# Graph network in one kernel: PSUM operands and TensorE transposes in layer 0's edge loop, two PSUM tiles and a later last product at the end of layer 2, and earlier loads at the seams

## The chip, the cores and the metric

The kernel runs on one core of a Trainium2 chip, as one program. The metric is the device time of that core in microseconds (us), the median of several executions. Executions of the same kernel differ by some 0.1 to 0.3% on one chip. All runs told here are of the fast state: none is over 1.5% above the fastest of its kernel. Names of engines in the profile: PE is TensorE's matmuls, PEld its weight loads, DVE is VectorE, ACT ScalarE, POOL GpSimd, SP SyncE.

## The reference

A graph network of four layers over 4,096 nodes of 512 features and 65,536 edges. Each layer adds its result to `x` after a layer norm and a relu.

```python
h = relu(layernorm(x)); x = x + softmax(gat(h, adj, W, a))          # layer 0: 8 heads of 64, attention over the edges
h = relu(layernorm(x)); x = x + gcn(h, weight)                      # layer 1: degree-normed sum over edges, product, relu
h = relu(layernorm(x)); x = x + edge_mlp(h, edge_attr, W1 .. W4)    # layer 2, below
h = relu(layernorm(x)); x = x + relu(gcn(h @ W.T + b))              # layer 3

def edge_mlp(x):                                                    # layer 2
    hid = mish(concat(x[src], x[dst], edge_attr) @ W1 + b1)         # per edge
    agg = segment_sum(mish(hid @ W2 + b2), dst)                     # per edge, summed per node
    u   = mish(concat(x, agg) @ W3 + b3)                            # per node from here
    y   = x + u @ W4 + b4
    return layernorm(y) * gamma + beta
```

## The kernel before

Edges are sorted by node and taken in tiles of 128. The rows at the far ends of a tile's edges are gathered from DRAM by an indirect DMA that GpSimd issues, weighted, and added per node by a TensorE product with a one-hot matrix. In layer 0 a group is eight tiles. Three parts matter here. The first is **layer 0's loop**, which also needs each edge's own scores. It gets them from a product with the transposed one-hot, built on VectorE from a loaded table, `places`.

```python
def source_parts(g, places):
    oh_t = ep.tile([P, GT * P], BF16, name="oh_t")
    nc.vector.tensor_scalar(oh_t, places, col_i, None, op0=OP.is_equal)
    # ... of = three bf16 parts of the block's node scores ...
    for j in range(GT):
        for k in range(3):
            nc.tensor.matmul(e_ps[:, j]..., oh_t[:, j * P:(j + 1) * P], of[:, j // 2, k, :], start=k == 0, stop=k == 2)

def weights(g, rows, u):
    nc.vector.tensor_mul(rows[:, :, D:D + H], u, s_new[...])        # weights, into SBUF
    return one_hots(ep, s_loc, at(g), GT)                           # compare row_i (SBUF) with s_loc

def weigh(j, rows):                                                 # two tiles
    # ... ScalarE scales two of the eight heads ...
    nc.vector.tensor_mul(g, g, two[:, :, D:D + VH]...to_broadcast([P, 2, VH, F]))   # all operands in SBUF
```

The second is the **end of layer 2**, a software pipeline over 16 groups of 256 nodes:

```python
for p in range(groups + 3):
    if now(p):      # load rows of h2, transpose them and acc's on TensorE, copy out on ScalarE (h_t, a_t)
    if now(p - 1):  # product with w3
        u_ps = lps.tile([P, KC, R * P], F32, name="u_ps", bufs=1)
        for m in range(KC):
            for k in range(2 * KC):
                nc.tensor.matmul(u_ps[:, m, :], w3_sb[...], ..., start=k == 0, stop=k == 2 * KC - 1)
            nc.scalar.activation(zu[:, m, :], u_ps[:, m, :], AF.Identity, bias=b3_sb[:, m:m + 1])
    if now(p - 2):  # product with w4, o_ps, added to h2's rows
    if now(p - 3):  # last product: transposes of h3, copy to h3_t, product with wl, store to ztab
    if now(p - 2):  # layer norm of y, x3, layer norm of x3 -> h3
```

The third is the **seams**: what GpSimd and the loads do between layer 1 and the messages of layer 2 (edge ends are gathered only once layer 1 is over), and between the messages and layer 2's end (its weights and rows are loaded once all of the messages' memory is free).

Of the kernel before, what the change touches and what calls it, by code (L numbers as in the profile page):

```python
# [19 lines left out]
P = 128  # L20
# [13 lines left out]
def kernel(  # L34
# [54 lines left out]
    col_i = const.tile([P, 1], F32, name="col_i")  # L89
    nc.gpsimd.iota(col_i, pattern=[[0, 1]], base=0, channel_multiplier=1,  # L90
                   allow_small_or_imprecise_dtypes=True)
# [27 lines left out]

    loc_rows = dram.tile([G * P, P], BF16, name="loc_rows")  # L120
# [9 lines left out]
    def by_order(o, pool, ppool):  # L130
# [117 lines left out]
        nc.vector.tensor_tensor(limit, til[:1, :], limit, op=OP.is_gt)  # L248
        nc.vector.reduce_max(over, limit, axis=AX.X)
# [66 lines left out]
        low_p = pool.tile([P, G, P], BF16, name="low_p")  # L316
        nc.vector.tensor_copy(low_p, loc)
        nc.sync.dma_start(loc_rows.rearrange("(g p) c -> p g c", p=P), low_p)
# [132 lines left out]
    def one_hots(pool, loc, t0, n):  # L451

        oh = pool.tile([P, n, P], F32, name="oh")
        nc.vector.tensor_tensor(oh, row_i.unsqueeze(1).to_broadcast([P, n, P]),
                                loc[:, t0:t0 + n].unsqueeze(2).to_broadcast([P, n, P]), op=OP.is_equal)
        return oh
# [221 lines left out]
    def attend(first, last):  # L678
        @with_exitstack
        def run(ctx):  # L680
            ep = ctx.enter_context(tc.tile_pool(name="edge", bufs=2))
            eps = ctx.enter_context(tc.tile_pool(name="edge_ps", bufs=2, space=PSUM))
            groups = (last - first) // GT
# [11 lines left out]
            def fetch_places(g):  # L695
                places = ep.tile([P, GT * P], BF16, name="places", bufs=3)
                nc.sync.dma_start(places, loc_rows[at(g):at(g) + GT].rearrange("t c -> (t c)").partition_broadcast(P))
                return places

            def source_parts(g, places):  # L700

                oh_t = ep.tile([P, GT * P], BF16, name="oh_t")
                nc.vector.tensor_scalar(oh_t, places, col_i, None, op0=OP.is_equal)
                e_ps = eps.tile([P, GT, 2, H], F32, name="e_ps")
                of = ep.tile([P, GT // 2, 3, 2 * H], BF16, name="of")
                for j in range(0, GT, 2):
                    b = block_of(nc.scalar, bi_s, at(g) + j)
                    nc.scalar.copy(of[:, j // 2], node3[:, ds(b, 1)].rearrange("p b k c -> p (b k) c"))
                for j in range(GT):
                    for k in range(3):  # L710
                        nc.tensor.matmul(e_ps[:, j].rearrange("p c h -> p (c h)"), oh_t[:, j * P:(j + 1) * P],
                                         of[:, j // 2, k, :], start=k == 0, stop=k == 2)
                return e_ps

            def scores(rows, e_ps):
                u = ep.tile([P, GT, H], F32, name="u")
                nc.vector.tensor_add(u, e_ps[:, :, 0, :], rows[:, :, D:D + H])
                nc.vector.scalar_tensor_tensor(u, u, 0.2, u, op0=OP.mult, op1=OP.max)
                nc.vector.tensor_sub(u, u, e_ps[:, :, 1, :])

                nc.vector.tensor_scalar(u, u, SAFE_RANGE + 10.0, None, op0=OP.min)
                nc.scalar.activation(u, u, AF.Exp)
                nc.scalar.copy(rows[:, :, D + H:], one2.unsqueeze(1).to_broadcast([P, GT, 2]))
                return u

            def weights(g, rows, u):
                nc.vector.tensor_mul(rows[:, :, D:D + H], u,
                                     s_new[:, at(g):at(g) + GT].unsqueeze(2).to_broadcast([P, GT, H]))
                return one_hots(ep, s_loc, at(g), GT)

            def weigh(j, rows):
# [6 lines left out]
                g = two[:, :, :VH * F].rearrange("p t (h f) -> p t h f", h=VH)  # L738
                nc.vector.tensor_mul(g, g, two[:, :, D:D + VH].unsqueeze(3).to_broadcast([P, 2, VH, F]))
# [14 lines left out]
            rows, places, done = {}, {}, {}  # L754
            for g in range(-3, groups):
                now = lambda k: 0 <= k < groups
                if now(g + 3):
                    rows[g + 3] = fetch(g + 3)
                if now(g + 2):
                    places[g + 2] = fetch_places(g + 2)  # L760
                if now(g + 1):
                    e_ps = source_parts(g + 1, places.pop(g + 1))
                ps = None
                for j in range(0, GT, 2):
                    if now(g):
                        weigh(j, rows[g])
                        if ps is not None:
                            keep(g, j - 2, ps)
                        ps = add_up(g, j, rows[g], done[g])
                    if j == 2 and now(g + 1):  # L770
                        u = scores(rows[g + 1], e_ps)
                if now(g + 1):
                    done[g + 1] = weights(g + 1, rows[g + 1], u)
                if now(g):
                    keep(g, GT - 2, ps)
                    del rows[g], done[g]
# [81 lines left out]
    class Between:  # L858


        AHEAD, APART = 3, 8
# [13 lines left out]
        def block(self, b):  # L875
# [30 lines left out]
            for k0, tab in ((0, ptab), (KC, qtab)):  # L906
# [5 lines left out]
                pq = pool.tile([P, D], F32, name="pq", bufs=3)  # L912
# [29 lines left out]

    with tc.tile_pool(name="between", bufs=1) as bp, tc.tile_pool(name="between_ps", bufs=1, space=PSUM) as bps, \
# [3 lines left out]
                  between.follow)(0, TS_MAIN)  # L947
        between.the_rest()
    for flag in (more, late):
        with tc.If(nc.values_load(flag[:, 0:1], min_val=0, max_val=1) > 0):  # L950
            if flag is more:
                sum_edges(ytab, s_dst, s_loc, bi_s, 2)(TS_MAIN, TS)
            with tc.tile_pool(name="redo", bufs=1) as bp, tc.tile_pool(name="redo_ps", bufs=1, space=PSUM) as bps:
                Between(bp, bps).the_rest()
# [6 lines left out]

    half_pi = const.tile([P, 1], F32, name="half_pi")
# [3 lines left out]
    nc.gpsimd.memset(acc[:, NB // 2:, :D], 0.0)  # L966

    with ExitStack() as l2:
        wp = l2.enter_context(tc.tile_pool(name="l2_w", bufs=1))
# [7 lines left out]
        def messages(ctx, first, last):  # L977
            lp = ctx.enter_context(tc.tile_pool(name="l2", bufs=2))
            lps = ctx.enter_context(tc.tile_pool(name="l2_ps", bufs=2, space=PSUM))
            U = 4  # L980
            NG = (last - first) // U


            HALF = DE + 3
# [5 lines left out]
            def fetch_ends(i):  # L990
                eg = lp.tile([P, U // 2, 2 * HALF], F32, name="eg", bufs=4)
                for j in range(U):
                    t = first + i * U + j
                    nc.gpsimd.indirect_dma_start(  # L994
                        out=eg[:, j // 2, (j % 2) * HALF:(j % 2 + 1) * HALF], out_offset=None,
                        in_=aug.rearrange("e c -> (e c)").unsqueeze(0),
                        in_offset=bass.IndirectOffsetOnAxis(ap=d_eid[:, t:t + 1], axis=1))
                return eg

            def fetch_rows(eg):  # L1000
                pg = lp.tile([P, U, D], F32, name="pg", bufs=4)
                qg = lp.tile([P, U, D], F32, name="qg", bufs=3)
                for j in range(U):
# [4 lines left out]
            def keep_ends(i, eg):  # L1008
                r = slice(first + i * U, first + (i + 1) * U)
# [5 lines left out]
            def turn_attributes(eg):  # L1015
                et_ps = lps.tile([P, U // 2, P], F32, name="tr_ps")
                for j in range(U // 2):
                    nc.tensor.transpose(et_ps[:, j, :], eg[:, j, 3:3 + 2 * DE], ident)
                et = lp.tile([P, U // 2, P], F32, name="et")
# [3 lines left out]
            def attribute_products(et):  # L1023
                made = []
                for j in range(U):
# [23 lines left out]




            fetched, rows, h, z = {}, {}, {}, {}
            ctx.enter_context(tc.manual_schedule(engines=ENGINES))
            for i in range(-3, NG + 2):
                now = lambda k: 0 <= k < NG
                if now(i + 3):
                    fetched[i + 3] = fetch_ends(i + 3)
# [3 lines left out]
                if now(i - 1):  # L1062
                    hh = h.pop(i - 1)
                    zz = z[i - 1] = lp.tile([P, U, D], F32, name="z", bufs=2)
# [12 lines left out]
                if now(i - 2):  # L1077
                    oh = one_hots(lp, d_loc, first + (i - 2) * U, U)
                    mz = z.pop(i - 2)
                    t = lp.tile([P, U, D], F32, name="t", bufs=1)  # L1080
# [3 lines left out]
                if now(i - 1):  # L1084
                    ps = second_product(h_t[1])
                    nc.vector.tensor_add(zz[:, 1, :], ps, b2_bc)  # L1086
                if now(i + 1):
# [4 lines left out]
                if now(i):  # L1092
# [5 lines left out]
                if now(i + 1):  # L1098
                    for j in range(2, U):
# [4 lines left out]
                if now(i - 2):  # L1104
                    nc.scalar.activation(t, t, AF.Sin, bias=half_pi, scale=-2.0)
                    for j in range(0, U, 2):
                        nc.vector.tensor_mul(mz[:, j:j + 2], mz[:, j:j + 2], t[:, j:j + 2])  # L1107
                if now(i):
# [5 lines left out]
                for j in range(U):  # L1114
                    if now(i - 2):
                        add_message(first + (i - 2) * U + j, oh[:, j, :], mz[:, j, :])
                    if now(i) and j == 1:
                        nc.vector.tensor_mul(pg[:, 2:], pg[:, 2:], qg[:, 2:])

        in_two(1, TD_MAIN, TD, messages)  # L1120
# [3 lines left out]
    with ExitStack() as end:  # L1124
        wp = end.enter_context(tc.tile_pool(name="l2_end_w", bufs=1))
        lp = end.enter_context(tc.tile_pool(name="l2_end", bufs=2))
        lps = end.enter_context(tc.tile_pool(name="l2_end_ps", bufs=2, space=PSUM))
        w3_sb = load_w(wp, "w3_sb", w3)
        w4_sb = load_w(wp, "w4_sb", w4)
        wl_sb = load_w(wp, "wl_sb", w_l3t)  # L1130
# [193 lines left out]
```

## Time and profile before

The median of the kernel before was 6323.75 us in its first three runs. I use stages between landmarks that both traces have, since the same work then stands on both sides:

| stage, between starts in the trace | before, us |
|---|---|
| to layer 0's first product of the loop (`sum_ps`) | 297.3 |
| layer 0's loop, first to last `sum_ps`, 68 groups | 755.4 |
| last `qtab` store (layer 1 over) to the messages' first product (`m_ps`) | 53.7 |
| messages, first to last `m_ps` | 2919.5 |
| last `m_ps` to the first product of layer 2's end (`u_ps`) | 46.6 |
| layer 2's end, first `u_ps` to the last store of `ztab` | 585.4 |
| from there to the end of the span | 694.2 |

Each row is the difference of two starts. The view of one tile gives them: for each operation the count, the shortest, median and longest duration in ns, then the first and the last start.

```profile
L745 PE MATMUL sum_ps<-rows,oh x2176: 381/383/782, 297.3 to 1052.7; 128*128 128x261 f32 x198
```

1052.7 less 297.3 is the loop's 755.4 us, 11.1 a group. In a group's line, "x529 | 572.6, 1082 | 161.2 <-issue 130.1" means 529 instructions, busy 572.6 us, 1,082 ns each, and an idle engine for 161.2 us in front of them, of which 130.1 with no cause that the profile shows.

### The profile page before, as it was taken

How to read it: one execution, taken by the hardware profiler on the slowest of the kernel's cores; microseconds unless marked ns; L12 is line 12 of the kernel's file. 1: busy time of each engine (PE TensorE's matmuls, PEld its weight loads, DVE VectorE, ACT ScalarE, POOL GpSimd, SP SyncE). 2: the span in 40 equal slices, each digit the busy share in tenths (PEclk: the TensorE clock that was granted, in tenths of full speed). 3: DMA queues.
4: the chain of work that ended last, by engine and by line, in shares of the span. 5: the costliest groups of instructions: out<-in, count | busy, mean ns of one | idle time of the engine just before them, and what ended most of it. 6: DMA issues, size and time to landing. Idle time of an engine off the chain costs nothing. (4 is left out here: it accounts for less than half of the span.)

```text
span 6333.0 us, 65970 instructions
## 1 busy us (share of the span) xinstructions
PE 5615.5 (89%) x18462; PEld 2821.0 (45%) x18462; DVE 4171.6 (66%) x7268; ACT 2953.4 (47%) x4025; POOL 3262.4 (52%) x3295
## 2 busy tenths in 40 slices
PE   6688887899998899999999999999999789968877
PEld 4366665344443344444444444444444465632222
DVE  7577778466654666666666666666666445556666
ACT  3144444311110677777777777777777533310000
POOL 1277774276774755555555555555555000027776
PEclk9799999999999999999999999999999899989999
DMA  8777775587785433333333333333333211137777
GB/s 227 175 217 214 217 216 180 183 244 234 240 235 171 126 99 102 103 103 101 100 101 99 99 103 103 103 100 100 101 99 100 78 47 63 61 109 210 225 242 220
DMA packets 401315, 926.61 MB, mean 146 GB/s; under 512 B 137462, under 2 KB 137462, under 8 KB 400918
## 3 DMA queue, kind: packets, MB, share of 16 engines
q0 software_dynamic: 230976, 721.66, 39.6%
q1 hardware_dynamic: 169942, 200.40, 10.0%
q8 instruction: 159, 2.61, 0.2%
q14 instruction: 238, 1.95, 0.1%
HBM read 818.71 MB, written 103.11 MB: 146 GB/s over the span
## 5 line engine op out<-in xcount | busy, mean ns | idle before, releaser
L448 PE MATMUL m_ps<-w_sb,h_t 128*128 128x512 f32 x4224 | 1905.3, 599 | 31.2 <-ACT h_t L1037 31.2
L813 PE MATMUL sum_ps<-g,oh 128*128 128x512 f32 x2144 | 1075.0, 617 | 157.7 <-DMA g<-ztab,d_src 94.3
L448 PEld LDWEIGHTS m_ps<-w_sb,h_t 128*128 128x128 f32 x4224 | 770.9, 190 | 983.3 <-issue 790.8
L459 POOL DMA_INDIRECT qg<-qtab,eg x528 | 503.3, 953 | 990.1 <-ACT h_t L1037 845.2
L459 POOL DMA_INDIRECT g<-ztab,d_src x528 | 514.2, 974 | 867.5 <-DMA x_end<-x 706.9
L469 DVE TENSOR_TENSOR acc<-acc,sum_ps 128x512 f32 x800 | 549.8, 687 | 535.6 <-PE sum_ps L813 453.3
L459 POOL DMA_INDIRECT g<-ytab,s_dst x544 | 541.0, 994 | 402.8 <-DMA x_mid<-x 187.1
L813 PEld LDWEIGHTS sum_ps<-g,oh 128*128 128x128 f32 x2144 | 376.8, 192 | 796.4 <-DVE acc L469 346.6
L459 POOL DMA_INDIRECT rows<-htab,s_dst x544 | 587.1, 1079 | 209.3 <-issue 134.4
L994 POOL DMA_INDIRECT eg<-aug,d_eid x528 | 568.9, 1078 | 161.2 <-issue 137.1
L1037 ACT COPY h_t<-tr_ps 128x512 f32<-128x512 f32 x528 | 283.8, 589 | 777.2 <-PE tr_ps L1035 777.2
L745 PE MATMUL sum_ps<-rows,oh 128*128 128x261 f32 x2176 | 556.0, 412 | 58.0 <-PE sum_ps L745 41.4
L459 POOL DMA_INDIRECT pg<-ptab,eg x528 | 509.2, 964 | 160.9 <-issue 160.3
L745 PEld LDWEIGHTS sum_ps<-rows,oh 128*128 128x128 f32 x2176 | 430.4, 203 | 162.4 <-PE sum_ps L745 67.5
L1047 PE MATMUL small_ps<-z,oh 128*128 128x512 f32 x1056 | 477.5, 595 | 8.4 <-DVE z L1107 8.4
L1086 DVE TENSOR_TENSOR z<-m_ps,b_bc 128x512 f32<-128x512 f32 x132 | 91.3, 692 | 467.4 <-PE m_ps L448 467.4
L469 DVE TENSOR_TENSOR acc<-acc,small_ps 128x512 f32 x528 | 360.8, 683 | 31.5 <-PE small_ps L1047 4.1
L1262 ACT ACTIVATE t_end<-acc,dis 128x512 f32<-128x512 f32 x32 | 23.0, 721 | 664.7 <-DVE acc L469 664.7
L1072 DVE TENSOR_TENSOR z<-m_ps,b_bc 128x512 f32<-128x512 f32 x132 | 91.3, 692 | 352.2 <-PE m_ps L448 352.2
L1047 PEld LDWEIGHTS small_ps<-z,oh 128*128 128x128 f32 x1056 | 201.3, 191 | 263.6 <-issue 221.8
L1107 DVE TENSOR_TENSOR z<-z,t 128x1024 f32<-128x1024 f32 x264 | 310.2, 1216 | 8.2 <-ACTq L474 4.8
L1035 PEld LDWEIGHTS tr_ps<-ident,pg 128*128 128x128 f32 x2112 | 247.8, 141 | 151.2 <-issue 120.2
(266 smaller groups left out, 8471.7 us busy)
## 6 DMA issues: line engine op xcount, KB each, us to landing
aug<-row SPq DMA_DIRECT2D x32, 560.0 KB, 4.7
places<-loc_rows SPq DMA_DIRECT2D x68, 256.0 KB, 4.0
xt<-in_x_dram SPq DMA_DIRECT2D x16, 1024.0 KB, 6.7
row<-in_edge_attr_dram SPq DMA_DIRECT2D x32, 512.0 KB, 6.7
rows<-htab,s_dst POOLq DMA_INDIRECT x544, 3.8
g<-ytab,s_dst POOLq DMA_INDIRECT x544, 4.3
eg<-aug,d_eid POOLq DMA_INDIRECT x528, 2.7
pg<-ptab,eg POOLq DMA_INDIRECT x528, 3.6
```

Of the source, the lines that this page charges most:

```text
L448: nc.tensor.matmul(ps, h_t[:, k, :], w_sb[:, k0 + k, :], start=start and k == 0, stop=stop and k == KC - 1)
L459: nc.gpsimd.indirect_dma_start(out=dst_ap, out_offset=None, in_=table, in_offset=bass.IndirectOffsetOnAxis(ap=idx, axis=0))
L469: nc.vector.tensor_add(into, into, ps)
L745: nc.tensor.matmul(ps[:, c, :HW], oh[:, j + k, :], rows[:, j + k, c * HW:(c + 1) * HW], start=k == 0, stop=k == 1)
L813: nc.tensor.matmul(ps, oh[:, j + k, :], g[:, j + k, :], start=k == 0, stop=k == pair - 1)
L994: nc.gpsimd.indirect_dma_start(out=eg[:, j // 2, (j % 2) * HALF:(j % 2 + 1) * HALF], out_offset=None, in_=aug.rearrange("e c -> (e c)").un ...
L1035: nc.tensor.transpose(h_ps[:, k, :], h[:, j, k * P:(k + 1) * P], ident)
L1037: nc.scalar.copy(h_t, h_ps)
L1047: nc.tensor.matmul(ps, oh, m, start=True, stop=True)
L1072: nc.vector.tensor_add(zz[:, 0, :], ps, b2_bc)
L1086: nc.vector.tensor_add(zz[:, 1, :], ps, b2_bc)
L1107: nc.vector.tensor_mul(mz[:, j:j + 2], mz[:, j:j + 2], t[:, j:j + 2])
```

## The change

Its intent: shorten layer 0's loop by giving VectorE's large operations a PSUM operand and taking the transposed one-hots from TensorE; keep TensorE fed at layer 2's end; and start loads and gathers earlier at the seams. The core of the diff, with cuts marked:

```diff
 # layer 0's loop
+both_ps = kept.tile([P, P + 2 * GT * H], F32, name="both_ps")    # PSUM: row ids, and two slots of weights
+nc.scalar.copy(ids_ps, row_i)
-places = ep.tile([P, GT * P], BF16, name="places", bufs=3)        # and its load
-nc.vector.tensor_scalar(oh_t, places, col_i, None, op0=OP.is_equal)
+nc.tensor.transpose(t_ps[:, k, :], oh[:, j + k, :], ident)        # eight a group, then two ScalarE copies to bf16
-for k in range(3): nc.tensor.matmul(e_ps[:, j]..., of[:, j // 2, k, :], ...)      # 24 products of 16 columns
+nc.tensor.matmul(e_ps[:, j]..., of[:, j // 2]..., start=True, stop=True)          # 8 products of 48 columns
+nc.vector.reduce_sum(near, e_ps..., axis=AX.X)
-nc.vector.tensor_mul(g, g, two[:, :, D:D + VH]...)
+nc.vector.tensor_mul(part, part, w_ps[:, g % 2, j:j + 2, :VH]...)
 # ... and a new order of the steps of three groups ...
 # seam ahead of the messages
+begun = {i: fetch_ends(0, i) for i in range(3)}                   # edge ends, while layer 1 still runs
-nc.gpsimd.memset(acc[:, NB // 2:, :D], 0.0)
+nc.scalar.activation(acc[:, NB // 2:, :D], zero..., AF.Copy)
 # ... first multiply after Sin ahead of the next group's additions; one branch fewer after layers 1 and 3 ...
 # layer 2's end
+own = dict(reuse_waits="tile")                                    # pools wait for the bytes of a tile, not for all
+# w3 in halves between the first two groups' rows, wl last
-u_ps = lps.tile([P, KC, R * P], F32, name="u_ps", bufs=1)
+u_ps = [lps.tile([P, KC // 2, R * P], F32, name="u_ps") for _ in range(2)]
-for m in range(KC):
+for m in (0, 2, 1, 3):
+nc.gpsimd.tensor_add(h[p], h[p], b4_bc...)                        # was on VectorE; so with beta
-if now(p - 3):                                                    # last product
+if now(p - 4):                                                    # ... at the end of the body
 # ... norms with 13 tiny operations instead of 15, scale and gamma in one pass ...
```

## The prediction

> **What bounds the kernel now.** I first cut the span into stages with the table of busy time by stretch. Its columns: length; then busy us and instructions (x) of TensorE, its weight loads, VectorE, ScalarE and GpSimd; granted clock; DMA share; GB/s. The rows are layer 0's edge loop, layer 1's edges, layer 2's messages, layer 2's end and layer 3's edges.
>
> ```profile
> 280.00:1065.00 785.00, 607.90 (x3808) 476.06 (x3808) 598.20 (x1041) 337.55 (x1502) 587.05 (x544) 0.93 0.75 212
> ...
> 1222.00:2050.00 828.00, 739.37 (x1829) 331.81 (x1829) 497.32 (x1082) 107.36 (x243) 557.02 (x557) 0.96 0.75 228
> 2050.00:5030.00 2980.00, 2877.84 (x8712) 1334.57 (x8712) 2030.50 (x2772) 2157.64 (x1720) 1576.69 (x1579) 0.99 0.34 100
> 5030.00:5660.00 630.00, 522.44 (x1937) 341.10 (x1938) 308.72 (x842) 192.84 (x224) 12.53 (x13) 0.94 0.20 70
> 5660.00:6333.00 673.00, 542.32 (x1040) 163.08 (x1039) 449.84 (x683) 22.99 (x32) 501.68 (x515) 0.99 0.75 223
> ```
>
> The messages, nearly half of the time, keep TensorE 97% busy, and the diff leaves their steady loop alone. The two other edge loops are not touched either. What can move is layer 0's loop, layer 2's end, and the seams on both sides of the messages.
>
> In layer 0's loop no engine looks full, so I read its groups of instructions by line, then the instructions in order of time, then the clock microsecond by microsecond.
>
> ```profile
> L459 POOL DMA_INDIRECT rows<-htab,s_dst x529 | 572.6, 1082 | 161.2 <-issue 130.1 <-PE sum_ps L745 14.6 <-DVE u L719 7.9
> ```
>
> ```profile
> 612.64 0.54 DVE L703 TENSOR_SCALAR oh_t<-places,col_i 128x1024 bf16<-128x1024 bf16 x1
> ...
> 613.10 1.81 DVE L739 TENSOR_TENSOR rows<-rows 128x768 f32<-128x768 f32 x2
> ...
> 613.24 1.62 POOL L459 DMA_INDIRECT rows<-htab,s_dst  x1 [0.30 <-issue]
> ...
> 617.66 0.95 POOL L459 DMA_INDIRECT rows<-htab,s_dst  x1 [0.30 <-DMA rows<-htab,s_dst]
> 617.86 0.70 DVE L752 TENSOR_TENSOR acc<-acc,sum_ps 128x522 f32 x1 [2.95 <-PE sum_ps L745]
> ```
>
> ```profile
> 615.00:616.00 1.00, 1.00 (x3) 0.71 (x3) 0.00 (x0) 0.00 (x0) 0.83 (x1) 0.50 0.90 243
> ```
>
> GpSimd issues 8 gathers a group, each 1.082 us plus a gap of 161.2/529 = 0.305: 8 x 1.387 = **11.1 us**. The loop's period is the same: its first and last products start 755.2 us apart over 68 groups, 11.1 each. So GpSimd's issue sets the pace. A gather takes 0.95 us, but 1.62 beside VectorE work that reads SBUF only, and it ends when that work does; beside an addition that reads PSUM (L752) it stays at 0.95. TensorE loses too: after its idle time before the small score products the clock is 0.50 for some 3 us of each group.
>
> In layer 2's end TensorE is the bound, with named holes; the seam ahead of it waits for loads that begin only when the messages are over:
>
> ```profile
> L1191 PE MATMUL u_ps<-h_t,w_sb 128*128 128x256 f32 x512 | 128.6, 395 | 30.0 <-ACT zu L1193 30.0
> ...
> L448 PE MATMUL o_ps<-wl_sb,h_t 128*128 128x512 f32 x256 | 117.6, 613 | 17.9 <-ACT h_t L1171 17.9
> ...
> L1169 PE MATMUL tr<-ident,h 128*128 128x128 f32 x128 | 18.8, 292 | 24.3 <-DVE h L1161 24.3
> ```
>
> ```profile
> 5047.70 1.94 PE L1169 MATMUL tr<-ident,h_sb 128*128 128x128 f32 x8 [22.41 <-DMA h_sb<-h]
> ```
>
> **What the Trainium skill says.** "GPSIMD Engine Reference", section 1: GpSimd's SBUF interface is shared with VectorE, with contention from instructions in a 2-port mode or with two SBUF inputs. The lines above agree (1.62 against 0.95). "VectorE: DVE Perf Modes", "Why PSUM operands drop a tier": a PSUM operand holds fp32 work to one element a cycle, which `tensor_tensor` has anyway. The trace agrees: 522 elements with a PSUM operand take 694 ns, 768 from SBUF alone 951, both near 1 ns an element beyond a fixed part. "TensorE: Matmul & The Clock Gate", Part 1: an idle window of about 3.4 us halves the clock. Here 0.50 lasts about that long. Its Part 4 says that transposes do not count as busy in the same way; in the messages, with 18 transposes a group, the clock is 0.99.
>
> **Layer 0's loop.** Removed: the load of `places`, the 0.54 us comparison and 16 of 24 score products. Moved to PSUM operands: the one-hot comparison (1.22 us) and four weighings (0.95 each), so that 5.5 us of locks a group are nearly gone. Added: eight transposes (1.04 us for eight, by the messages' rows), two ScalarE copies, a reduction. GpSimd then needs 8 x (0.945 + 0.305) = 10.0 us. TensorE warm: 32 product records at 3.76 us per 16 = 7.5; transposes 1.04; eight score products about 0.45 (24 narrower ones take 0.76; estimate). And one wait: in the changed order VectorE does, between the scores and the last product, the reduction (about 0.55, estimate), four small ops (0.9), a weighing (0.95) and an addition (0.69), 3.1 us, beside a product of 1.9: 1.2 idle. Sum **10.2**. VectorE's own sum stays near 8.9. TensorE's 10.2 is the larger: 0.9 x 68 = **-60 us**.
>
> **Seam before the messages.** Ahead of the first row gather (2053.9) GpSimd spends 6.9 us on clearing `acc` and 8 x 1.25 on edge-end gathers. Both go: three groups of ends are fetched before the seam, ScalarE clears. But all engines must pass the second branch, and ScalarE's clear of 8192 elements takes about 7.6 us (an estimate: four times the 1.9 us that its passes over 2048 take in the messages). I take -10. The first multiply after Sin now precedes the second group's additions: Sin ended at 2075.85, the multiply began at 2084.19, -8. Sum **-18**.
>
> **Seam after them.** The last addition into `acc` ends at 5026.05, the first product of the end starts at 5053.4. With weights and rows in place earlier, two rounds of transpose (1.0 to 1.9) and copy (1.02) remain, some 5 us: **-22**.
>
> **Layer 2's end.** Two PSUM tiles by turns put another 3.6 us product over each 0.56 us wait: -28 of the 30.0. The last product a group later fills the waits for the final norms: -24. Against it, one more iteration early on has nothing to cover the load of rows (4.65 us seen before a transpose at 5104): +5. The 17.9 us wait for `h_t` stays, as the product still follows its own transposes. Shorter norms and the bias additions on GpSimd lie beside TensorE (VectorE is 55% busy): 0. Sum **-47**. One branch fewer at the end: -3.
>
> Sum: -60 - 18 - 22 - 47 - 3 = -150, so 6323.75 - 150 = **6174 us** (2.4%).
>
> **Rivals.** (1) GpSimd stays the bound: if the few small ops still lock it, or the shared pace slips, the loop is at 10.6 rather than 10.2: -33 instead of -60, 6200. For: it is the pace now, and 10.0 is close. (2) TensorE goes cold in the new loop, because transposes do not count: some 1.7 us a group, no gain there, 6235. Against: 0.99 in the messages. (3) VectorE and TensorE overlap better than my order of work and GpSimd's 10.0 binds, and layer 2's end hides `h_t` as well: 6140. (4) DMA takes over: the gathers move 8 x 128 x 2080 bytes in 10.2 us, 209 GB/s, under the 212 that the stage moves now; unlikely.
>
> **Range and chances.** Layer 0's loop is the wide term: -20 if a part of its gain is lost to a new wait, -75 if the loop runs at GpSimd's 10.0. The other three were worked out from single waits, and I allow each 8 us, partly cancelling. From 6174 that gives 6138 to 6212. Faster by over 2% needs under 6197, 23 us above my number, so three of the four terms may miss a third of their size before it fails: 0.83. Slower by over 2% would need layer 0's loop at 14 us a group, for which I see no mechanism.
>
> **What would show it.** Gathers of `rows` near 0.96 us instead of 1.08; a period of 10.2 with a granted clock near 0.98; TensorE's largest wait there before the last product, on VectorE. First message product some 36 us after the last store of `qtab` is issued, not 54; first product of the end within 8 us of the last addition; waits on `zu` near zero, those on `h_t` still near 18. I am wrong if gathers are short but the period stays at 11, or if the clock in the loop falls under 0.93.

## The result, and the profile after

The changed kernel took **6144.28 us** (median of 4 runs, 6142.68 to 6148.06) against 6326.26 for the kernel before on the same chip: ratio 0.9714 (95% interval 0.9697 to 0.973), **2.9% faster**. A ratio is the mean time of one kernel's fast runs over that of the other's of the same rounds, so not quite the ratio of the medians. The profiled spans are 6333.0 and 6143.0 us.

| stage | before | after | difference | predicted |
|---|---|---|---|---|
| to the first `sum_ps` | 297.3 | 292.6 | -4.7 | 0 |
| layer 0's loop | 755.4 | 678.6 | -76.8 | -60 |
| last `qtab` store to first `m_ps` | 53.7 | 40.0 | -13.7 | -18 |
| messages | 2919.5 | 2920.8 | +1.3 | 0 |
| last `m_ps` to first `u_ps` | 46.6 | 21.4 | -25.2 | -22 |
| layer 2's end | 585.4 | 517.3 | -68.1 | -47 |
| to the end | 694.2 | 689.1 | -5.1 | -3 |

The stages left out of the table (between the loop and the last `qtab` store) add 2. The same table of stretches as in the prediction, now of the changed kernel; the rows are again layer 0's loop, layer 1's edges, the messages, layer 2's end and layer 3's edges:

```profile
276.00:975.00 699.00, 581.77 (x3264) 480.03 (x3264) 597.49 (x1021) 443.24 (x1702) 514.56 (x544) 0.98 0.75 209
...
1951.00:4935.00 2984.00, 2882.63 (x8739) 1337.95 (x8738) 2037.26 (x2773) 2167.24 (x1724) 1569.26 (x1573) 0.99 0.35 102
4935.00:5458.00 523.00, 490.28 (x1902) 334.29 (x1900) 291.79 (x722) 191.70 (x223) 74.62 (x32) 0.99 0.18 65
```

These stretches are cut roughly, and the one of layer 2's end before holds 23 us of the idle seam. Cut at the landmarks of the stages, with the same view: in layer 0's loop VectorE is busy for 584.6 us before and 591.7 after, though the loop is 77 us shorter, and the clock goes from 0.94 to 0.99; in layer 2's end the clock goes from 0.97 to 0.99, and TensorE's busy time falls from 507.0 to 488.7 us for the same 1890 records. The groups of layer 0's loop that answer to the gather line of before, by line:

```profile
L760 PE MATMUL sum_ps<-rows,oh 128*128 128x261 f32 x2176 | 527.2, 390 | 109.8 <-issue 101.9 <-DVE rows L753 7.9
L452 POOL DMA_INDIRECT rows<-htab,s_dst x532 | 503.2, 946 | 162.1 <-issue 129.5 <-PE sum_ps L760 14.3 <-DMA rows<-htab,s_dst 7.6
```

A gather takes 0.946 us, not 1.082; the gap ahead of it is the same, 162.1/532 = 0.305. Eight take 8 x 1.251 = 10.0 us, and the loop's period is 678.6/68 = 9.98. The longest of these gathers took 1.003 us. TensorE now waits 110 us, 1.6 a group. The instructions in order of time show a weighing with a PSUM operand and a gather side by side:

```profile
603.21 1.81 DVE L753 TENSOR_TENSOR rows<-rows,both_ps 128x768 f32<-128x768 f32 x2
603.29 0.95 POOL L452 DMA_INDIRECT rows<-htab,s_dst  x1 [0.30 <-issue]
```

Two weighings in a row (1.81 us) leave the gather at 0.95; before, such a gather took 1.62. In layer 2's end, the groups:

```profile
L1254 PE MATMUL u_ps<-h_t,w_sb 128*128 128x256 f32 x512 | 122.2, 382 | 0.0
...
L441 PE MATMUL o_ps<-wl_sb,h_t 128*128 128x512 f32 x256 | 114.1, 599 | 18.0 <-ACT h_t L1231 18.0
...
L1229 PE MATMUL tr<-ident,h_sb 128*128 128x128 f32 x128 | 18.4, 292 | 9.1 <-DMA h_sb<-h 9.1
```

The waits on `zu` are gone, the ones on `h_t` are as they were, and 9.1 us of waits for rows of `h2` remain.

### The profile page after: what moved, and what is told of

Its sections match the earlier page's. It is cut to its first block, busy times and chain, and to the rows that moved or that the text cites. A ratio compares the mean times of both kernels' runs of the same rounds, so it can differ in the third digit from the quotient of the medians.

```text
span 6143.0 us, 65022 instructions
## 1 busy us (share of the span) xinstructions
PE 5565.5 (91%) x17918; PEld 2825.7 (46%) x17918; DVE 4167.2 (68%) x7156; ACT 3069.3 (50%) x4232; POOL 3254.2 (53%) x3326
## 5 line engine op out<-in xcount | busy, mean ns | idle before, releaser
L760 PE MATMUL sum_ps<-rows,oh 128*128 128x261 f32 x2176 | 527.2, 390 | 109.8 <-issue 101.9
L452 POOL DMA_INDIRECT rows<-htab,s_dst x544 | 514.6, 946 | 205.0 <-issue 132.8
L760 PEld LDWEIGHTS sum_ps<-rows,oh 128*128 128x128 f32 x2176 | 398.1, 190 | 192.4 <-issue 127.5
```

The source lines that it names most:

```text
L452: nc.gpsimd.indirect_dma_start(out=dst_ap, out_offset=None, in_=table, in_offset=bass.IndirectOffsetOnAxis(ap=idx, axis=0))
L760: nc.tensor.matmul(ps[:, c, :HW], oh[:, j + k, :], rows[:, j + k, c * HW:(c + 1) * HW], start=k == 0, stop=k == 1)
```

## The experiments

Twelve kernels were run, in three sessions, each on another chip; each session has its own runs of the kernel before (medians 6335.9, 6334.0 and 6331.3 us). Intervals of the ratios are some 0.0015 to each side, 10 us. The stage lengths are sharper: layer 0's loop took 678.6 to 680.9 us in all nine traces that have the changed loop untouched, and layer 2's end 516.4 to 517.6 in all seven that have the changed end untouched. So I argue from stages and give the ratio beside them. All results passed the check, even that of `seven`, whose edit loads wrong rows on purpose: the check did not notice them.

**The theory.** In layer 0's loop GpSimd's issue of gathers sets the pace, and VectorE work that reads only SBUF holds gathers up. **Rivals:** the gain is TensorE's (new order, fewer products, warm clock) or the missing loads'; or TensorE with its wait is the bound (my prediction's own step).

### only_l0: the kernel before with the changed loop alone

```diff
 # kernel before, with the changed attend(), one_hots(); without loc_rows, col_i
```

> The kernel before with the changed layer 0 loop alone. If the parts of the change are independent, the loop's products start 679 us apart from first to last instead of 755, the stage ahead of it is 3 to 4 us shorter, and nothing behind it moves: some 80 us less than the kernel before, 6246. Rival: part of the loop's gain in the whole change comes from elsewhere (DMA traffic, pools): then less than 60 of the 80 us show here.

Measured: ratio 0.9877 (0.986 to 0.9893), 6254.61 us. The loop took 679.0 us, the end of layer 2 585.6 as before. The loop's gain is its own, and the parts add up. The stage ahead of the loop, 297.3 before and 292.6 after, was 291.0 to 298.1 in the thirteen traces with the changed preparation, so its 4.7 us are not a finding.

### both_sbuf, ids_sbuf, w_sbuf: operands back in SBUF

```diff
-ohs[g + 2] = one_hots(ep, s_loc, at(g + 2), GT, 3, ids_ps)
+ohs[g + 2] = one_hots(ep, s_loc, at(g + 2), GT, 3)                      # ids_sbuf, both_sbuf
-                     w_ps[:, g % 2, j:j + 2, :VH].unsqueeze(3)...
+                     rows[:, j:j + 2, D:D + VH].unsqueeze(3)...         # w_sbuf, both_sbuf
```

> The changed kernel with the one-hot comparison's row ids and the weighing's factors read from SBUF again; order of work, transposes and score products as changed. Theory (VectorE work that reads SBUF only holds up GpSimd's gathers, and GpSimd's issue is the pace): gathers near 1.06 us instead of 0.946, period near 10.9 instead of 9.98, some 60 us more than the changed kernel, 6205. Rival (the gain is TensorE's: new order, fewer score products, warm clock, no places load): gathers may change, but the time stays within 10 us of 6144.

> The changed kernel with the row ids of the one-hot comparison in SBUF again, the weighing's factors still in PSUM. Theory (a gather is held up in proportion to the VectorE time that reads SBUF only; both operands in SBUF cost 1.5 us a group over 5.0 us of such work): the comparison's 1.22 us cost 0.37 a group, gathers near 0.99, loop 25 us longer than the changed kernel's 679. Rival (a lone operation hides in the 0.305 gap or under TensorE's own 9.8): under 8 us.

> The changed kernel with the weighing's factors read from SBUF, the row ids in PSUM. Theory (in proportion, 3.8 of 5.0 us): 1.1 us a group, gathers near 1.085, loop 755, 76 us longer than the changed kernel's 679. Rival (the comparison, one long operation, is the costly one): under 50 us here and over 50 with the row ids alone.

The gathers in each, by line, in the same order as above:

```profile
L452 POOL DMA_INDIRECT rows<-htab,s_dst x540 | 612.5, 1134 | 164.5 <-issue 130.4 <-PE sum_ps L760 18.0 <-DVE both_ps L739 5.5
```

```profile
L452 POOL DMA_INDIRECT rows<-htab,s_dst x538 | 541.8, 1007 | 163.9 <-issue 132.8 <-PE sum_ps L760 17.4 <-DVE u L731 6.1
```

```profile
L452 POOL DMA_INDIRECT rows<-htab,s_dst x538 | 596.0, 1108 | 164.0 <-issue 131.7 <-PE sum_ps L760 16.8 <-DMA rows<-htab,s_dst 4.6
```

| operands in SBUF | gather, ns | 8 x (gather + gap), us | period, us | loop, us | ratio to before |
|---|---|---|---|---|---|
| none (the change) | 946 | 10.0 | 9.98 | 678.6 | 0.9714 |
| row ids | 1007 | 10.5 | 10.47 | 711.9 | 0.9767 |
| weights | 1108 | 11.3 | 11.26 | 765.8 | 0.9836 |
| both | 1134 | 11.5 | 11.47 | 780.3 | 0.986 |

The period follows eight gathers and their gaps to 0.04 us in every row. That alone says little, as lengths and gaps of an engine that does nothing else always add up to the period. What makes GpSimd the pace is the gap: from 300 to 960 us none of the gathers in these four traces, nor in that of the kernel before, starts over 0.35 us after the end of the one ahead of it. Whatever cause is printed for such a gap, it is some 0.30 us long, so the gathers wait for no other engine. VectorE's own operations are as long as before (a weighing 953 ns with both in SBUF, 947 in the change), so it is the gathers, and not VectorE, that grow. The TensorE rival falls: with order, transposes and score products all as changed and without the loads of `places`, the loop with both operands in SBUF takes 25 us longer than the loop of before. So the PSUM operands are worth 102 us, and the rest of the loop's change gives 25 of it back. In the same 660 us 43% of the gathers there take over 1.0 us, 26% in the kernel before and none in the change. Why more are held there than before (means of 1134 and 1082 ns) these runs don't tell; I had expected 1060. The shares do not add up either: 33 and 87 us apart, 102 together.

### seven: an eighth of the gathers issued by another engine

```diff
-for j in range(GT):
+for j in range(GT - 1):
     gather(rows[:, j, :D + H], htab, ...)
+nc.sync.dma_start(rows[:, GT - 1, :D + H], htab[:P])      # as many bytes; wrong rows on purpose
```

> The changed kernel with the eighth of each group's gathers replaced by a plain load of as many bytes that another engine issues: wrong result on purpose. GpSimd needs 7 x 1.25 = 8.75 us a group instead of 10.0. Theory (GpSimd's issue is the pace, TensorE's wait ahead of the last product is slack): the period falls towards TensorE's own 9.0, at least 0.6 us a group less, 40 to 65 us in all, 6080 to 6105. Rival (my prediction's step: TensorE with its wait needs 10.2 and binds): the period stays within 0.2 of 9.98 and the time within 15 us of 6144.

Measured: ratio 0.9693, 6141.75 us; the loop 665.8 us, 9.79 a group. By the limits set beforehand the rival came true, barely: the period fell by 0.19 us (limit 0.2), and the time is 2 us from 6144, 13 by the ratio (limit 15). My theory's gain of 40 to 65 us did not come. But the rival's mechanism falls too, as TensorE with its wait cannot need 10.2 us in a period of 9.79. What is left: GpSimd is the pace of the change, by only 0.19 us a group, 13 us in all. Here it does wait, with a gap above 0.35 us in 56 of the 464 gathers from 300 to 960 us, and its waits name TensorE:

```profile
L452 POOL DMA_INDIRECT rows<-htab,s_dst x473 | 448.4, 948 | 200.6 <-issue 120.6 <-PE sum_ps L761 74.5 <-DMA rows<-htab,s_dst 2.4
```

And TensorE, in order of time over one group:

```profile
608.97 2.00 PE L761 MATMUL sum_ps<-rows,oh 128*128 128x261 f32 x8 [1.32 <-issue]
610.81 1.04 PE L701 MATMUL t_ps<-ident,oh 128*128 128x128 f32 x8
611.68 3.69 PE L761 MATMUL sum_ps<-rows,oh 128*128 128x261 f32 x16
615.21 0.36 PE L720 MATMUL e_ps<-of,oh_t 128*128 128x48 bf16 x8
615.41 2.01 PE L761 MATMUL sum_ps<-rows,oh 128*128 128x261 f32 x8
618.81 2.00 PE L761 MATMUL sum_ps<-rows,oh 128*128 128x261 f32 x8 [1.39 <-issue]
```

From start to start the eight products take 1.84 us, the transposes 0.87, sixteen products 3.53, the score products 0.20: each line's length includes a tail that the next line overlaps. The last eight take 2.01 and TensorE then waits 1.39: work of 8.45 and a wait of 1.4, 9.8 in all. That wait stands ahead of the group's last eight products, and VectorE's last weighing (0.95 us from 617.15) is not what ends it. Behind it comes the addition that frees the PSUM tile for them, until 618.70; ScalarE's scaling of the same rows had ended at 618.58:

```profile
618.01 0.69 DVE L768 TENSOR_TENSOR acc<-acc,sum_ps 128x522 f32 x1
```

VectorE is busy for 8.84 of these 9.84 us. So TensorE and VectorE together look like the next bound; no run tried that alone.

### u_one: the w3 product in one PSUM tile again

```diff
-u_ps = [lps.tile([P, KC // 2, R * P], F32, name="u_ps") for _ in range(2)]
-for m in (0, 2, 1, 3):
+u_ps = lps.tile([P, KC, R * P], F32, name="u_ps", bufs=1)
+for m in range(KC):
```

> The changed kernel with u_ps in one PSUM tile again. Theory (a wait of 0.56 us in the profile costs TensorE 0.83, [...]three times a group): layer 2's end 2.5 us a group longer, 40 us in all, 557 instead of 517 from the first product to the last store. Rival (my prediction's step: only the wait as printed): 28 us.

Measured: ratio 0.9771; the end 561.6 us, **44.3 more** than the change's 517.3. The group and two of its products in order of time:

```profile
L1254 PE MATMUL u_ps<-h_t,w_sb 128*128 128x256 f32 x512 | 129.1, 396 | 30.0 <-ACT zu L1256 30.0
```

```profile
5200.73 1.99 PE L1254 MATMUL u_ps<-h_t,w_sb 128*128 128x256 f32 x8 [0.56 <-ACT zu L1256]
...
5205.01 1.99 PE L1254 MATMUL u_ps<-h_t,w_sb 128*128 128x256 f32 x8 [0.56 <-ACT zu L1256]
```

One m takes 4.28 us from start to start with a printed wait of 0.56; in the change the same sixteen matmuls take 3.45. So a wait of 0.56 costs 0.83: it is printed from the end of the line before, whose last 0.16 us (1.89 long, 1.73 from start to start) the next line otherwise overlaps, and the eight matmuls behind it take 1.83 to the next start instead of 1.73. Three a group over 16 groups make 40 us, and the stores to `ztab` agree: 34.05 us apart here, as in the kernel before, and 31.55 in the change. The other 4 us come from the start of the stage (first product to first store 129.0 us, 114.7 in the change, of which 10 are counted already), where I did not take them apart.

### wl_early: the last product at its old place

```diff
-for p in range(groups + 4):
+for p in range(groups + 3):
-    if now(p - 4):          # last product, at the end of the body
+    if now(p - 3):          # last product, ahead of the norms
```

> The changed kernel with the last product at its old place, one group earlier. Theory (the drain's two waits of 8.7 and 15.6 us come back, and the clock goes to 0.7 to 0.8 behind them): the end 25 to 30 us longer, the last two groups' products at 0.55 us instead of 0.44 us a matmul's issue, granted clock under 0.8 in the last 50 us. Rival (the shorter norms and the additions on GpSimd have taken those waits away by themselves): under 12 us.

Measured: ratio 0.9735; the end 536.8 us, **19.5 more**. Between both theories. The last two groups on TensorE, and the last 50 us of the stage in the table of stretches:

```profile
5439.51 2.12 PE L1229 MATMUL tr<-ident,h 128*128 128x128 f32 x8 [6.45 <-DVE h L1221]
...
5466.24 2.12 PE L1229 MATMUL tr<-ident,h 128*128 128x128 f32 x8 [13.31 <-DVE h L1221]
```

```profile
5430.00:5480.00 50.00, 26.23 (x56) 11.78 (x54) 24.14 (x79) 4.80 (x6) 0.00 (x0) 0.69 0.08 32
```

The waits of the drain, the last groups in which no other product fills them, come back, 19.8 us in all, and with them a clock of 0.69; the eight transposes take 2.12 us instead of 1.04. The waits are shorter than the 24.3 of before; the norms ahead of them are shorter now, which may be why, but was not tried alone. The waits for `h_sb` are 4.6 us here, 9.1 in the change.

### h3_ahead: the last product's transposes earlier

```diff
+if now(p - 4):
+    h3_t = turned("h3_t", h3.pop(p - 4), AF.Relu)       # between the w3 and the w4 product
 if now(p - 2):
     # ... w4 product ...
 if now(p - 4):
-    h3_t = turned("h3_t", h3.pop(p - 4), AF.Relu)
```

> The changed kernel with the transposes of the last product's rows moved ahead of the product with w4, so that ScalarE's copy lies beside that product. Theory (the 18.0 us that TensorE waits for h_t in layer 2's end are all on the path): that wait goes to below 3, the end stage is 15 us shorter, 6129. Rival (the wait is slack that comes back before u_ps or u_t): under 5 us.

Measured: ratio 0.9684 (0.9668 to 0.97), 6134.3 us; the end 499.7 us, 17.6 less than the change. The group of the last product, whose wait was 18.0:

```profile
L441 PE MATMUL o_ps<-wl_sb,h_t 128*128 128x512 f32 x256 | 112.8, 593 | 3.8 <-ACT h_t L1231 2.3 <-DVE acc L1274 1.4
```

The wait that the change left in place was all on the path: the printed waits fell by 14.2 us and the stage by 17.6, so a wait seems to cost more than its printed length here too: the change's groups are 31.55 us apart, these 30.17.

### plain_pools: pools that wait for all of their memory

```diff
-own = dict(reuse_waits="tile")
+own = {}
```

> The changed kernel with the pools of layer 2's end waiting for the whole of the memory that they take over, as before, loads in the changed order. Theory (weights and first rows can start only when every user of the messages' pools is done): last message product to first product of the end 46 us instead of 21, 25 us more in all. Rival (the order and halving of the loads did it): under 8 us more.

Measured: ratio 0.9725; last `m_ps` to first `u_ps` 30.8 us instead of 21.4, so **9.4 us, not 25**. The first transpose of layer 2's end shows what it waits for:

```profile
4943.39 1.94 PE L1229 MATMUL tr<-ident,h_sb 128*128 128x128 f32 x8 [7.51 <-DMA h_sb<-h]
```

My expectation missed. Of the seam's 25.2 us, 9.4 belong to the finer waits. The other 15.8 are left, by difference, to the rest that changed there, above all the new order of loads (half of `w3` and the first rows ahead of the other weights); that was not tried alone. The same seam took 43.7 us in only_l0, which does not touch it, against 46.6 in the one trace of the kernel before, so some 3 us of this may be chance.

### no_begun: edge ends gathered at the seam again

```diff
-begun = {i: fetch_ends(0, i) for i in range(3)}
-messages(0, TD_MAIN, begun)
+messages(0, TD_MAIN)
```

> The changed kernel without the prefetch of three groups of edge ends; clear of acc by ScalarE, first multiply after Sin and the branch's place as changed. Theory: eight gathers of edge ends at 1.25 us lie ahead of the first row gather again, 20 to 23 us after the last store of qtab instead of 12.5; first message product 8 to 10 us later, 8 to 10 us in all. Rival (another wait, for the stored tables or the branch, ends later anyway): under 4 us.

Measured: ratio 0.9729. GpSimd's first instructions after the seam:

```profile
1965.01 0.94 POOL L987 DMA_INDIRECT eg<-aug,d_eid  x1 [60.09 <-DVEq L1165]
...
1973.74 0.94 POOL L987 DMA_INDIRECT eg<-aug,d_eid  x1 [0.30 <-issue]
1974.99 0.95 POOL L452 DMA_INDIRECT pg<-ptab,eg  x1 [0.30 <-issue]
```

Eight gathers of ends precede the first row gather, which comes 22.4 us after the last store of `qtab` (at 1952.6) instead of 12.5; the first product comes 48.3 after it instead of 40.0. The prefetch is worth 8 us there. The messages took 2925.2 us as well, where the other traces with the changed messages have 2919.4 to 2921.0: TensorE waits for the second group too (2.58 us before a transpose at 2023.47), so some 4 us more belong to the prefetch.

### adds_dve: bias additions on VectorE again

```diff
-nc.gpsimd.tensor_add(h[p], h[p], b4_bc...)
+nc.vector.tensor_add(h[p], h[p], b4_bc...)             # and beta into xs
```

> The changed kernel with the two bias additions of layer 2's end on VectorE again. Theory (VectorE is under 60% busy there and TensorE is the bound): tiny VectorE operations of the norms become shorter without GpSimd beside them, the end's length from first product to last store within 5 us of 517. Rival (the additions' place on VectorE delays the sums that free the rows' buffers): over 8 us more.

Measured: ratio 0.9712; the end 516.7 us against 517.3. Nothing. Where the additions run makes no difference to the time, though it does to VectorE. The norm's first multiply in the change, then here:

```profile
L1209 DVE TENSOR_SCALAR down<-st 128x2 f32<-128x2 f32 x32 | 28.5, 892 | 1.1
```

```profile
L1209 DVE TENSOR_SCALAR down<-st 128x2 f32<-128x2 f32 x32 | 5.4, 169 | 1.1
```

The 892 ns are a mean of two lengths. In the change 21 of these operations, on two elements a partition, take 0.17 us, and 11 take 2.27 us; those 11 start beside an addition of GpSimd's and end about when it ends:

```profile
5170.71 2.34 POOL L1266 TENSOR_TENSOR xs<-xs,beta_bc 128x1024 f32<-128x1024 f32 x1
5170.81 2.27 DVE L1209 TENSOR_SCALAR down<-st 128x2 f32<-128x2 f32 x1
```

With the additions on VectorE all 32 take 0.17. All of it lies beside TensorE.

### better: h3_ahead and a fourth buffer for h2's rows

```diff
-t = lp.tile([P, R, D], F32, name="h2_sb", bufs=3)
+t = lp.tile([P, R, D], F32, name="h2_sb", bufs=4)
 # and h3_ahead's edit
```

> The changed kernel with two edits in layer 2's end: the last product's transposes ahead of the product with w4 (as h3_ahead), and four buffers instead of three for the rows of h2, so that the third and fourth group's rows need not wait for the first group's last reader. Theory: waits on h_t and on h_sb both go; beside the 18 us of h3_ahead another 9.1 us of waits and the cold clock behind them, 12 us; the end 487 us from the first product to the last store, 30 us less than the changed kernel, ratio to the kernel before 0.967. Rival (the rows then wait for the vector additions or the DMA instead): 499 as in h3_ahead.

Measured, in five rounds: **6114.36 us**, ratio **0.966 (0.9647 to 0.9673)** to the kernel before; its interval lies below that of the change (0.9697 to 0.973). The end took 485.8 us, 31.5 less than the change and 13.9 less than h3_ahead.

```profile
L1229 PE MATMUL tr<-ident,h_sb 128*128 128x128 f32 x128 | 16.6, 273 | 0.0
```

The 9.1 us of waits for `h_sb` are gone, and with them the transposes at half speed (a mean of 273 ns instead of 292). This version beats both kernels.

## Why the prediction was right or wrong

The time is inside the range, near its lower edge, and the direction is right. The gain was larger than predicted: 182 us by the medians and 190 by the profiled spans, against 150; the profiled execution of the kernel before was a longer one (6334.85 us) than its timed ones. Most of the difference lies in two terms. That the time is so near rival 3's 6140 is partly luck: its first half came true (GpSimd binds), its second did not (the wait on `h_t` is still 18.0 us), and another error, in the cost of waits, made up for it.

**Layer 0's loop, -77 instead of -60.** The mechanism was right: three runs with operands put back move the period with the length of the gathers. The step that failed is "TensorE's 10.2 is the larger". The sum took each line's printed length (7.5 + 1.04 + 0.45 = 9.0), and these lengths overlap; start to start the same work takes 8.45. The wait was estimated at 1.2 and is 1.4. With seven gathers TensorE and VectorE came down to 9.8, so GpSimd's 10.0 binds, the first half of rival 3. Rival 1, that small operations still hold up gathers, is refuted by 946 ns; rival 2, the cold clock, by 0.98 in the stretch and 1.00 from 300 to 960 us (the prediction's reading of the clock before was thin: the idle time ahead of the 3 us at 0.50 is printed as 1.29 us, so no idle stretch of 3.4 us stands there); rival 4 by a DMA share of 0.75 as before. The Trainium skill, "GPSIMD Engine Reference", section 1, names contention from instructions with two SBUF inputs, and the runs agree (a gather of 1134 ns with both operands in SBUF, 946 with them in PSUM).

**Layer 2's end, -68 instead of -47.** The two-tile step, "-28 of the 30.0", was mis-sized: it counted the wait as printed, and each costs 0.83 us rather than 0.56. Undoing it costs 44. "The last product a group later" was put at -24 and +5, -19 net; undoing it costs 19.5. The +5 is there too: waits for `h_sb` are 9.1 us in the change and 4.6 with the last product at its old place. That the 17.9 us wait on `h_t` stays was right, and that the additions on GpSimd change nothing too. The remaining 4 of the 68 us (68.1 - 44.3 - 19.5) were not tried alone; the norms may be in them.

**Seam ahead of the messages, -14 instead of -18.** Its first part, -10, was -7.8 (first row gather 20.3 us after the last store of `qtab` before, 12.5 after). The second, -8, was -5.9 (gather to product 33.4, then 27.5). The multiply does begin right behind Sin now, at 1990.23, where Sin runs from 1988.20 for 2.00. ScalarE's clear took 7.03 us, estimated at 7.6. Why the first part fell short shows in no_begun, which keeps the clear's move and the branch and only undoes the prefetch: its first row gather comes 22.4 us after the last store, later than the 20.3 of before, although GpSimd no longer clears for 6.9 us. It waits for the branch until 12.4 us after the store. So the prefetch made the gain, and what the clear's move freed the wait for the branch took back.

**Seam after the messages, -25 instead of -22.** The size was right. The prediction did not separate finer waits from the order of loads, and my later guess gave all of it to the waits; they have 9.4. The first product starts 3.2 us after the last addition ends (4933.4), under the 5 that were left for it.

**One branch fewer, -3, measured -5.1.** Not shown. From the last store of `ztab` to the end, only_l0, which has both branches, took 689.7 us, inside the 687 to 692 of the runs with one.

## What to carry to other kernels

If an engine that issues gathers sets the pace, measure the single gather beside what the other engines do: with one operand of the large VectorE operations in PSUM instead of SBUF a gather took 0.95 us instead of 1.13 and the loop 102 us less, though the VectorE operations themselves were no shorter. Count the cost of a short wait on TensorE from start to start, not from the printed idle time, and sum busy times the same way. After a change, read the waits that it left: two small edits to those of layer 2's end gave another 31 us.

## What the Trainium skill lacked or had wrong

- Neither "GPSIMD Engine Reference", section 1, nor "SBUF — State Buffer" has a figure for a gather's issue beside `tensor_tensor` operations with two SBUF operands, or tells that it is lengthened: 946 ns with a PSUM operand in all large VectorE operations, 1007, 1108 and 1134 with one or both operands in SBUF.
- Neither has a figure for very small VectorE operations beside GpSimd: those on two elements a partition took 2.27 us beside one of its additions and 0.17 without.
- "TensorE: Matmul & The Clock Gate", Part 4, says that the full clock does not engage for transposes. Here eight took 1.04 us at a granted clock of 1.00, and 2.12 us at 0.50 behind a wait of 6.45 us, and a loop with eight of them a group ran at 1.00. Whether transposes count as busy these runs don't show, as products stand around them.
- No page that I read says what a short wait costs beyond its length: one of 0.56 us between two products cost 0.83 us from start to start.
